# Storing the last tile but one in two transfers of 1024 columns instead of four of 512

## The chip, the cores and the metric

One core of a Trainium2 chip runs the whole program. The metric is the device time of one execution in microseconds (us); the kernel before has a median of 319.64 us over four runs (319.51 to 319.73).

## The reference

The kernel adds to x (8 batches of 512 tokens, 2048 features, float32) the output of a routed low-rank layer. Its input is a linear layer with a low-rank adapter chosen for each batch; of the 8 experts, each token takes only the one with the highest logit, times that logit. Cut to what matters:

```python
# conditioning: x is (8, 512, 2048), W is (2048, 2048)
base_out = einsum('bti,oi->bto', x, W) + b
lora_h   = einsum('bti,bir->btr', x, lora_As[mapping])
y        = base_out + 2.0 * einsum('btr,bro->bto', lora_h, lora_Bs[mapping])
# routed low-rank layer: 8 experts of rank 16, best one only
logits = einsum('bsd,ed->bse', y, route_w)
topk_v, topk_idx = top_k(logits, 1)
route_weight = one_hot(topk_idx[..., 0], 8) * topk_v
h   = einsum('bsd,erd->bser', y, A)
out = x + einsum('bser,eor->bso', route_weight[..., None] * h, Bw)
```

## The kernel before

The layers in front of the routing are folded into one small matrix first: W times the 136 columns of A and of the router (128 of the experts, 8 logits), and for each batch the adapter's part is added. After that, each token needs only a product of its 2048 features with a 2048 x 136 matrix, the choice of the expert, and a product of 128 values with the 128 x 2048 matrix `fb`.

The 4096 tokens are 32 tiles of 128 rows (`NT` = 32), loaded in pairs (`TPU` = 2) into buffers of 128 x 2 x 2048. For each tile:

- POOL and ACT shuffle the loaded rows into quarters, and VectorE (DVE) transposes 32 x 32 blocks (`shuffle`, line 249, and `turn_x`, line 234).
- TensorE multiplies the 16 transposed blocks with the folded matrix (`heads`, line 452).
- DVE picks the expert and scales its 16 values (`route`, lines 463 to 473).
- TensorE transposes that (`turn_heads`, line 520), ACT copies it to SBUF (`keep_heads`, line 525).
- TensorE multiplies it with `fb`, 512 columns to a matmul (`delta`, line 558); DVE adds the product to the tile of x in place (`add_delta`, line 571); the tile is stored from there (`store`, line 580).

The order on each engine is the order in which the program issues the work. The loop at line 606 runs over half tiles: pass n computes half of tile n // 2's heads and the `delta` of an earlier half (`piece(n)`), and adds the half before that. A `delta` of one half is 1024 columns.

For tiles 0 to 29 a half is one PSUM tile of 1024 columns, added by one instruction, and the tile is stored whole (128 rows of 8 KB) after its second half. The last two tiles are listed in `ends` (line 536). Their halves are cut into pieces, each with a PSUM bank of its own, `pe_o`, `pe_h` or `pe_s` by the pool it is from:

```python
    ends = {
        (NT - 2, 0): (("o", 512), ("o", 512)),
        (NT - 2, 1): (("h", 512), ("s", 512)),
        (NT - 1, 0): (("h", 512), ("o", 512)),
        (NT - 1, 1): (("o", 512), ("h", 256), ("s", 256)),
    }
```

Each piece is added and stored by itself, so tile 30 leaves in four stores of 512 columns and tile 31 in three of 512 and two of 256. All stores of tile 30 are issued by SP; those of tile 31 by SP and ACT in turn within a half. `add_delta` may be told to handle only the first n pieces of a half; that is done once, at line 640, where the first piece of tile 30 is added one pass before the second. `po_tiles[t, h]` keeps the pieces that are still to be added.

SP issues all loads of x and nearly all stores, in program order. By line 606's last passes all loads have been issued. A store waits on SP for the DVE add of its columns, and then goes out. No later instruction of the kernel writes the columns of tile 30 again.

Of the kernel before, what the change touches and what calls it, by code (L numbers as in the profile page):

```python
# [18 lines left out]
def kernel(  # L19
# [32 lines left out]
    nc = tc.nc  # L52
# [3 lines left out]
    B, T, D = x.shape  # L56
# [9 lines left out]
    NT = B * TPB  # L66
# [369 lines left out]
    po_tiles = {}  # L436
# [90 lines left out]
    def bank(tag, n):  # L527
# [8 lines left out]
# [6 lines that stand above are left out]
# [22 lines left out]
    def add_delta(t, h, n=None):  # L564

        u, k = divmod(t, TPU)
        pieces = po_tiles[t, h]
        po_tiles[t, h] = pieces[n:] if n else []
        for m, (cols, part) in enumerate(pieces[:n]):
            xs = x_tiles[u][:, k, cols]  # L570
            nc.vector.tensor_tensor(xs, xs, part, ALU.add)  # L571
            if (t, h) in ends:
                store(t, cols, nc.scalar if t == NT - 1 and m % 2 else nc.sync)
            elif h == 1:
                store(t, ds(0, D))

    def store(t, cols, eng=nc.sync):
        u, k = divmod(t, TPU)
        b, r = divmod(t, TPB)
        eng.dma_start(out=out[b, ts(r, P), cols], in_=x_tiles[u][:, k, cols])  # L580
# [25 lines left out]
    for n in range(2 * NT + 4):  # L606
        t, h = divmod(n, 2)
# [7 lines left out]
        if tp >= 0 and not folds(n - 1):  # L615
            add_delta(tp, hp)
# [11 lines left out]
        if folds(n):  # L628
            pass
        elif n == 2 * NT:  # L630

            delta(*piece(n), lambda: turn_heads(t - 1))
        else:
            if folds(n - 1):
                delta(*piece(n - 1))
                add_delta(*piece(n - 1))
            if piece(n)[0] >= 0:
                delta(*piece(n))
            if n == 2 * NT - 1:
                add_delta(*piece(n), 1)  # L640
# [54 lines left out]
```

## Time and profile before

| what | value |
|---|---|
| median of 4 runs | 319.64 us (319.51 to 319.73) |
| the profiled execution's own time | 319.53 us |
| its span in the profile | 317.8 us |
| TensorE (PE) busy | 311.3 us, 98% |
| DVE / ACT / POOL busy | 239.4 / 188.1 / 163.5 us |
| HBM read / written | 54.60 / 33.55 MB |
| granted TensorE clock, mean | 1.0 |

The page's list of transfers, by line, engine, count, size of one and median time from issue to landing:

```profile
x<-in_x_dram SPq DMA_DIRECT2D x32, 1024.0 KB, 8.0
out_dram<-x SPq DMA_DIRECT2D x30, 1024.0 KB, 4.7
...
out_dram<-x SPq DMA_DIRECT2D x6, 256.0 KB, 2.6
...
out_dram<-x ACTq DMA_DIRECT2D x1, 256.0 KB, 2.4
```

The 30 stores of 1024 KB are tiles 0 to 29. Six of the 256 KB stores on SP and one on ACT are the pieces of tiles 30 and 31 with 512 columns; a row of such a piece is 2 KB in each of 128 partitions. A row of a whole tile is 8 KB. The program ends when all stores have landed.

### The profile page before, as it was taken

The page shows a single profiled execution, that of the slowest core. Times are in us where ns is not written, and L with a number is a line of the kernel's source. Part 1 is how long each engine was busy: PE and PEld are TensorE (multiplying, and loading weights), DVE is VectorE, ACT ScalarE, POOL GpSimd, SP SyncE. Part 2 cuts the span into 40 slices and gives each one's busy share as a digit, 9 for nine tenths or more (in the row PEclk, how much of TensorE's full clock was granted, in tenths as well). Part 3 has the DMA queues.
Part 4 walks back from the last instruction along what each step waited for, and adds up shares of the span by engine and source line. Part 5 has one row for each costly group of instructions (what it writes and reads, how often), then busy time and mean ns, then how long its engine had stood idle before and what let it go on. Part 6 is the DMA issues. An engine that isn't in the chain of part 4 may idle for free.

```text
span 317.8 us, 5569 instructions
## 1 busy us (share of the span) xinstructions
PE 311.3 (98%) x2140; PEld 246.1 (77%) x2140; DVE 239.4 (75%) x422; ACT 188.1 (59%) x245; POOL 163.5 (51%) x167
## 2 busy tenths in 40 slices
PE   7999999999999999999999999999999999999994
PEld 7999999999776767786777767767777777677762
DVE  2221699957988798879887987888888888888864
ACT  3322366848697497659765965677587749760000
POOL 1012095999994849094819553935397276710000
PEclk9999999999999999999999999999999999999999
DMA  7999999989323494959495858767685859444337
GB/s 283 410 363 415 419 421 422 416 323 403 142 101 165 168 362 173 375 205 385 146 399 187 352 170 359 249 282 257 273 325 206 329 231 363 168 168 169 162 149 249
DMA packets 15307, 88.52 MB, mean 279 GB/s; under 512 B 1696, under 2 KB 4016, under 8 KB 4912
## 3 DMA queue, kind: packets, MB, share of 16 engines
q1 hardware_dynamic: 14112, 85.45, 68.6%
q0 software_dynamic: 320, 2.11, 1.6%
q10 hardware_dynamic: 848, 0.61, 0.6%
q8 instruction: 17, 0.28, 0.4%
q14 instruction: 10, 0.08, 0.1%
HBM read 54.60 MB, written 33.55 MB: 277 GB/s over the span
## 4 chain that ended last, share of the span: by engine, by line
PE 96%; DMA 2%; DVE 1%; DVEq 0%; issue 0%
PE ph L452 38%; PE po L558 32%; PE pc L293 19%; DMA w<-in_w_dram 2%; PE po L349 2%; PE pg L333 1%; PE pw L520 1%; PE pe_o L558 1%; PE ph L349 1%; PE pe_h L558 1%; DVE x L571 0%; PE pc L349 0%; PE pe_s L558 0%; DVE m L370 0%; DVE wv L279 0%; DVEq L691 0%
## 5 line engine op out<-in xcount | busy, mean ns | idle before, releaser
L249 POOL COPY xq<-x 32x1024 f32<-32x1024 f32 x121 | 126.4, 1044 | 77.3 <-DVE wh L473 32.4
L249 ACT COPY xq<-x 32x1024 f32<-32x1024 f32 x135 | 140.9, 1043 | 14.7 <-DMA x<-in_x_dram 12.7
L452 PEld LDWEIGHTS ph<-m,xT 128*128 128x128 f32 x1024 | 124.8, 190 | 21.1 <-issue 15.8
L452 PE MATMUL ph<-m,xT 128*128 128x136 f32 x1024 | 129.7, 280 | 0.3 <-DVE m L370 0.3
L558 PE MATMUL po<-fb,whT 128*128 128x512 f32 x240 | 111.6, 592 | 0.0
L571 DVE TENSOR_TENSOR x<-x,po 128x1024 f32<-128x1024 f32 x60 | 72.9, 1216 | 28.2 <-PE po L558 27.9
L234 DVE STREAM_TRANSPOSE xT<-xq 128x1024 f32<-128x1024 f32 x64 | 78.8, 1235 | 2.4 <-POOL xq L249 1.8
L558 PEld LDWEIGHTS po<-fb,whT 128*128 128x128 f32 x240 | 41.7, 190 | 32.0 <-issue 31.8
L293 PE MATMUL pc<-pj,wv 128*128 128x136 f32 x512 | 59.9, 279 | 0.7 <-DVE wv L279 0.7
L293 PEld LDWEIGHTS pc<-pj,wv 128*128 128x128 f32 x512 | 59.5, 190 | 0.9 <-DVE wv L279 0.9
L525 ACT COPY whT<-pw 128x128 f32<-128x128 f32 x32 | 8.5, 265 | 56.9 <-PE pw L520 56.8
L279 ACT COPY wv<-w 128x1024 f32<-128x1024 f32 (+1 forms) x17 | 16.8, 996 | 30.1 <-DMA w<-in_w_dram 28.8
L279 DVE COPY wv<-w 128x1024 f32<-128x1024 f32 (+1 forms) x17 | 13.0, 771 | 25.6 <-DMA w<-in_w_dram 20.4
L515 POOL TENSOR_TENSOR m<-m,c 128x408 f32<-128x408 f32 x14 | 14.4, 1048 | 1.6 <-ACT m L510 1.1
L221 POOL COPY ad_q<-ad_ar 32x512 f32<-32x512 f32 x12 | 8.9, 744 | 9.6 <-DMA ad_ar<-in_cond_a_dram,arow_i 9.0
L508 DVE TENSOR_TENSOR m<-c,po 128x408 f32<-128x408 f32 x14 | 7.5, 575 | 5.2 <-PE po L349 5.2
L504 ACT COPY m<-ph 128x136 f32<-128x136 f32 x14 | 3.1, 275 | 13.8 <-PE pa L349 13.8
L463 DVE TENSOR_TENSOR ph<-ph,c0b 128x136 f32<-128x136 f32 x32 | 9.0, 282 | 1.8 <-PE ph L452 1.8
L391 POOL DMA_DIRECT2D bias_o<-in_bias_dram x1 | 0.7, 735 | 18.6 <-DVE bias_o L390 18.6
L520 PEld LDWEIGHTS pw<-ident,wh 128*128 128x128 f32 x32 | 4.5, 141 | 7.4 <-issue 7.2
L473 DVE TENSOR_TENSOR wh<-ph,rw 128x128 f32<-128x128 f32 x32 | 9.3, 291 | 1.1
L471 DVE TENSOR_SCALAR rw<-ph,win,top 128x8 f32<-128x8 f32 x32 | 9.1, 284 | 1.2
(70 smaller groups left out, 146.6 us busy)
## 6 DMA issues: line engine op xcount, KB each, us to landing
x<-in_x_dram SPq DMA_DIRECT2D x32, 1024.0 KB, 8.0
out_dram<-x SPq DMA_DIRECT2D x30, 1024.0 KB, 4.7
w<-in_w_dram SPq DMA_DIRECT2D x16, 1024.0 KB, 11.9
out_dram<-x SPq DMA_DIRECT2D x6, 256.0 KB, 2.6
fb<-in_ffn_b_dram SPq DMA_DIRECT2D x1, 1024.0 KB, 12.6
pj<-in_proj_dram SPq DMA_DIRECT2D x2, 272.0 KB, 12.3
out_dram<-x ACTq DMA_DIRECT2D x1, 256.0 KB, 2.4
pj<-in_proj_dram SPq DMA_DIRECT2D x1, 204.0 KB, 9.4
```

Source lines behind the costliest of these rows:

```text
L234: nc.vector.transpose(dst[:, ts(h, HJ), :].rearrange("p j (g t) -> p g j t", t=Q), src.rearrange("p g (j a) -> p g j a", a=Q)[:, :, ts(h, ...
L249: copy(xq_tiles[u][ts(i, Q), :, g, :], x_tiles[u][ts(g, Q), :, ts(i, DQ)])
L279: copy(dst[:, ts(k, n)], wr[:, ds(h * HJ + k * n, n)])
L293: nc.tensor.matmul(pcs[z][:, n, :], wv_tiles[oc, j // HJ][:, j % HJ, :], pj[:, oc, :], start=(oc == 0 and n == 0), stop=(oc == NO - 1), sk ...
L349: nc.tensor.matmul(out, ad_q[ts(q, Q), b // 2, n, :], g4[ts(q, Q), b, :], start=start, stop=True, skip_group_check=not start, tile_positio ...
L452: nc.tensor.matmul(ph_tiles[t][:, :NP], xT_tiles[t][:, j, :], place(m, (j,))[:, 0, :], start=(j == 0), stop=(j == NJ - 1),)
L463: nc.vector.tensor_tensor(ph, ph, c0b, ALU.add)
L471: nc.vector.tensor_scalar(rw, key, win, top, ALU.is_equal, ALU.mult)
L473: nc.vector.tensor_tensor(wh.rearrange("p (e r) -> p e r", r=R), ph[:, :ER].rearrange("p (e r) -> p e r", r=R), rw.unsqueeze(2).to_broadca ...
L515: nc.gpsimd.tensor_tensor(place(m, js), place(m, js), place(cs, js), ALU.add)
L558: nc.tensor.matmul(part, whT_tiles[t], fb[:, ds(c, n)], start=True, stop=True)
L571: nc.vector.tensor_tensor(xs, xs, part, ALU.add)
```

## The change

Tile 31 is stored as before, piece by piece, on SP and ACT in turn. For tile 30 the four pieces are still computed and added one by one, but a store is issued only after the last piece of a half, and it covers the half: 1024 columns, 512 KB, rows of 4 KB, on SP. The condition asks that no piece of the half is left to be added and that this is its last one; so the piece that is added early at line 640 issues nothing. The other tiles' stores stay.

```diff
@@ -569,9 +569,11 @@
         for m, (cols, part) in enumerate(pieces[:n]):
             xs = x_tiles[u][:, k, cols]
             nc.vector.tensor_tensor(xs, xs, part, ALU.add)
-            if (t, h) in ends:
-                store(t, cols, nc.scalar if t == NT - 1 and m % 2 else nc.sync)
-            elif h == 1:
+            if t == NT - 1:
+                store(t, cols, nc.scalar if m % 2 else nc.sync)
+            elif (t, h) in ends and not po_tiles[t, h] and part is pieces[-1][1]:
+                store(t, ds(h * D // 2, D // 2))
+            elif (t, h) not in ends and h == 1:
                 store(t, ds(0, D))
```

## The prediction

> **What bounds the kernel now.** I read the page's chain first, then the end of the chain, then the last 10 us instruction by instruction, then the transfers of that stretch in quarter microseconds.
>
> The page: the profiled execution, and who stands on the chain that ends last.
>
> ```profile
> span 317.8 us, 5569 instructions
> ...
> PE 96%; DMA 2%; DVE 1%; DVEq 0%; issue 0%
> ```
>
> TensorE sets the time until its last matmul. The change touches neither a matmul nor what feeds one, so only what follows the last matmuls can move. Those last pieces of the chain are:
>
> ```profile
> 312.51 0.02 issue
> 312.54 1.02 DVE x L571 x2
> 313.56 0.33 DVEq L691
> ```
>
> The printed chain stops at 313.56 + 0.33 = 313.89 us, yet the span is 317.8. The 3.9 us after it hold no compute; what runs there is the last store. So the end is read from the stores. The adds that release the stores of the last tile but one (tile 30), and the issues of all stores of tiles 30 and 31 (start, length, engine):
>
> ```profile
> 307.96 1.27 DVE L571 TENSOR_TENSOR x<-x,pe_o 128x512 f32<-128x512 f32 x2
> 309.15 0.68 DVE L571 TENSOR_TENSOR x<-x,pe_h 128x512 f32<-128x512 f32 x1
> 309.96 0.69 DVE L571 TENSOR_TENSOR x<-x,pe_s 128x512 f32<-128x512 f32 x1
> ...
> 308.66 0.33 SPq L580 DMA_DIRECT2D out_dram<-x  x1
> 309.26 0.33 SPq L580 DMA_DIRECT2D out_dram<-x  x1
> 309.86 0.33 SPq L580 DMA_DIRECT2D out_dram<-x  x1
> 310.68 0.33 SPq L580 DMA_DIRECT2D out_dram<-x  x1
> 311.54 0.33 SPq L580 DMA_DIRECT2D out_dram<-x  x1
> 312.40 0.35 ACTq L580 DMA_DIRECT2D out_dram<-x  x1
> 313.25 0.33 SPq L580 DMA_DIRECT2D out_dram<-x  x1
> 313.59 0.35 ACTq L580 DMA_DIRECT2D out_dram<-x  x1
> 313.91 0.33 SPq L580 DMA_DIRECT2D out_dram<-x  x1
> ```
>
> The first four issues are tile 30 (I call them c0 to c3), the next five tile 31 (d0 to d4; d3 and d4 are 256 columns wide). The trace of the line gives their times from issue to landing: c0 2.4 us, c2 3.0, c3 2.7, d0 2.5, d1 2.4, d4 2.9. The last lands at 313.91 + 2.9 = 316.8, and closing the program takes the other 1.0 us to 317.8. A 256 KB store that meets nothing in its way needs 2.4 us (c0, d1); the smaller d4 needs 2.9, so at least 0.5 us of it is queueing. That is where an earlier store can reach the end. The transfers in stretches (the last two columns are the busy share of the 16 DMA engines, and GB/s; a share a little over 1 is a full engine whose packets overlap):
>
> ```profile
> 306.50:309.00 2.50, 2.50 (x8) 1.11 (x7) 2.33 (x8) 0.00 (x0) 0.00 (x0) 1.00 1.01 419
> 309.25:309.50 0.25, 0.25 (x2) 0.03 (x1) 0.25 (x1) 0.17 (x1) 0.00 (x0) 1.00 0.02 8
> 309.50:313.00 3.50, 3.50 (x11) 1.87 (x10) 2.86 (x5) 0.00 (x0) 0.00 (x0) 1.00 1.04 349
> 311.00:313.00 2.00, 2.00 (x8) 1.14 (x6) 1.66 (x3) 0.00 (x0) 0.00 (x0) 1.00 1.03 332
> 313.00:313.25 0.25, 0.25 (x2) 0.00 (x0) 0.25 (x2) 0.00 (x0) 0.00 (x0) 1.00 0.68 254
> 314.00:314.25 0.25, 0.00 (x0) 0.00 (x0) 0.00 (x0) 0.00 (x0) 0.00 (x0) 1.00 0.71 230
> ```
>
> Three things are to be seen. The DMA engines stand idle until 309.50, which is 0.84 us after the issue of c0: that is the time from an issue to its first data. From 309.50 they are full, at 349 GB/s for rows of 2 KB, where the store of tile 29 with rows of 8 KB ran at 419. And twice, at 313.0 and 314.0, they run dry for a moment: when d1 and d2 come, the queue is empty. What happens to tile 30 is therefore almost forgotten before the end, by a margin of a few tenths.
>
> **The change, part by part.** Both stores of tile 30 stay on SP, in the same places of its queue.
>
> *Removed:* two issues of 0.33 us on SP, and 256 of the 512 row packets of tile 30. SP is between waits for DVE there (it stands free from 308.66 + 0.33 = 308.99 to 309.26), so the issues are worth nothing. Without that cover, each would be worth at most its 0.33 us.
>
> *The wait that is added:* the store of the first half (call it A) now waits for the second add instead of the first. It is issued at 309.26, 0.60 us after c0. Queued behind it on SP are the second half (B) and the last tile's stores; B goes at 310.68, where c3 went, and waits for its own add anyway. No engine waits for SP: the tile's buffer isn't loaded again. The first matmul piece of tile 30, which is added early and alone, has no store of its own any more; that is the same 0.60. The adds and ACT's copies keep their times.
>
> *Transfer time.* By the full stretch, 256 KB take 262 KB / 349 GB/s = 0.75 us. No row of 4 KB stands in the trace, so the 512 KB of A is bounded from both sides: at the 2 KB rows' 349 GB/s it takes 1.50 us, at the 8 KB rows' 419 it takes 1.25. With a time per byte that is a constant and a cost per packet, 2 KB rows need 2.865 us per MB and 8 KB rows 2.387; the cost per packet at 8 KB is a third of the difference, 0.159, and at 4 KB twice that, so 2.387 + 0.159 = 2.546 us per MB and 1.33 us for 512 KB. I take 1.33.
>
> The Trainium skill speaks against any gain from longer rows: its page "DMA: Bandwidth & Descriptors", section "Where 436 GB/s comes from", says that between HBM and SBUF the HBM side binds at about 358 GB/s per core. The 419 GB/s of this trace's 8 KB rows stand above that, so the measurement decides; by the page the estimate for 512 KB would be 1.46 us and the sum below +0.47 instead of +0.26.
>
> *The queue, before:* data can start 0.84 us after each issue, and each 256 KB takes 0.75. c0 309.50 to 310.25, c1 to 311.00, c2 to 311.75, c3 to 312.50, d0 to 313.25, d1 to 314.00, d2 (can start 314.09) to 314.84. The two dips just where d1 and d2 start agree.
>
> *After:* A can start at 309.26 + 0.84 = 310.10 and ends 311.43. B can start at 311.52 and ends 312.85. d0, ready since 312.38, ends 313.60; d1 314.35; d2, ready since 314.09, ends 315.10. That is 0.26 us behind 314.84. d3 and d4 queue right behind d2 in both kernels, so the last landing and the end come 0.26 us later. The 0.60 us of the late start and 0.09 us of gap between A and B are paid back by 2 x (1.50 - 1.33) = 0.34 us of cheaper packets and by 0.09 us of slack before d2: 0.60 + 0.09 - 0.34 - 0.09 = 0.26.
>
> With 1.50 us for A: A ends 311.60, B 313.10, d2 315.35, so +0.51. With 1.25: B 312.77, d2 315.02, so +0.18. Below that the bound is about nothing: if d1 and d2 still meet an empty queue, the end is as before. A gain could come only from d2 to d4 being cheaper, and they are unchanged.
>
> The profiled execution has a span of 317.8 and took 319.53; with +0.26 it would be 319.79. The median of the four runs shown, 319.64, stands 0.11 above that execution, and the forecast is for a median: 319.64 + 0.26 = 319.90.
>
> **The rivals.** *Hidden altogether:* the queue is dry twice before the end, and if 512 KB go as fast as the best quarter microseconds of tile 29 (524 GB/s, 1.00 us), A ends 311.10, B 312.52, d2 314.86: +0.02, so 319.66. For it: the dips. Against it: 524 is a rate of quarters that others of 295 follow.
>
> *Slower:* the 4 KB rows don't go faster than the slowest full stretch shown, 332 GB/s over 311 to 313. Then A and B take 1.58 us each, B ends 313.26, d2 315.51: +0.67, so 320.31. It decides from 1.565 us per half (335 GB/s) on, where the sum reaches +0.64, which is 0.2%. For it: with a backlog nothing pays back the late start, and the two dips are means over 16 engines at 0.68 and 0.71, so some engines were busy all through them. Against it: the average row says 349, and longer rows have never been slower here.
>
> *Faster:* if all queueing of d4 vanished, its 2.9 us would become 2.4 at best, 0.5 us, so 319.14. For it: half the packets of tile 30. Against it: d2 to d4 themselves put 512 KB into the queue in 0.66 us, so they queue whatever tile 30 does. Even all of it isn't 0.2%.
>
> **How the numbers follow.** A measurement of this kernel can tell about 0.2%, 0.64 us, from no change; the bounds are 319.00 and 320.28. Forecast (+0.1 to +0.6) 0.52, hidden 0.19, slower 0.24, faster beyond 0.64 0.05. The first two lie within the bound and make 0.71. The range 319.5 to 320.45 takes in the bounds +0.18 and +0.51 and the slower rival's 320.31, with a little under the hidden case; the forecast's own range is 319.75 to 320.25.
>
> **What would show it right or wrong.** Right: A issued at about 309.26 and B at 310.68, the idle stretch of the DMA engines about 0.6 us longer, GB/s between 349 and 419 for A and B, no dips at 313.0 and 314.0 any more, d0 and d1 landing some 0.3 us later after issue than their 2.5 and 2.4, d4 about 0.3 later than its 2.9. Wrong: dips still there (hidden), or A and B at 335 GB/s or less and d4 landing 3.5 us or more after its issue (slower). If any matmul before 312 has moved, the whole reading is wrong.

## The result, and the profile after

The changed kernel takes 319.91 us (median of 40 runs, 319.70 to 320.32) against 319.61 of the kernel before on the same chips (60 runs, 319.42 to 319.89). The ratio is 1.001, 95% interval [1.0006, 1.0015]: slower by 0.30 us, between 0.2 and 0.5. So small a difference shows only over this many runs: it is half of the 0.2% that the prediction took for what can be told from no change.

The page of the changed kernel shows the same chain from the folding matmuls on, with a span 0.3 us longer, and the two stores that replace four:

```profile
span 318.1 us, 5565 instructions
...
PE 98%; DVE 1%; DVEq 0%; issue 0%
...
out_dram<-x SPq DMA_DIRECT2D x2, 512.0 KB, 2.6
out_dram<-x SPq DMA_DIRECT2D x2, 256.0 KB, 2.9
out_dram<-x ACTq DMA_DIRECT2D x1, 256.0 KB, 2.8
```

Of the stores of 256 KB that are left, d0 and d2 on SP have a median of 2.9 us to landing where c0 to d2 had 2.6, and d1 on ACT 2.8 where it had 2.4. They wait in a queue that was all but empty before. The issues of the changed kernel, in order: A, B, d0 to d4 (start, length, engine).

```profile
309.19 0.33 SPq L582 DMA_DIRECT2D out_dram<-x  x1
310.60 0.33 SPq L582 DMA_DIRECT2D out_dram<-x  x1
311.46 0.33 SPq L582 DMA_DIRECT2D out_dram<-x  x1
312.32 0.35 ACTq L582 DMA_DIRECT2D out_dram<-x  x1
313.18 0.33 SPq L582 DMA_DIRECT2D out_dram<-x  x1
313.51 0.35 ACTq L582 DMA_DIRECT2D out_dram<-x  x1
313.84 0.33 SPq L582 DMA_DIRECT2D out_dram<-x  x1
```

B and everything after it stand 0.08 us earlier than their counterparts before. That is the whole body of this execution: its first folding matmul (line 293) began at 6.32 us instead of 6.39. Over all profiles of this study it lies between 6.32 and 6.64, and the 307.5 us from there to the end of the last add are the same to some hundredths in all but two of them (0.1 and 0.2 longer). So tenths are best read from the last issue on. The transfers of the changed kernel by stretches (last two columns: busy share of the DMA engines, GB/s):

```profile
309.25:310.00 0.75, 0.75 (x3) 0.38 (x2) 0.62 (x2) 0.10 (x1) 0.00 (x0) 1.00 0.00 0
311.50:312.75 1.25, 1.25 (x6) 0.72 (x5) 0.98 (x2) 0.00 (x0) 0.00 (x0) 1.00 1.00 400
313.00:313.25 0.25, 0.25 (x2) 0.00 (x0) 0.25 (x2) 0.00 (x0) 0.00 (x0) 1.00 1.01 385
314.00:314.25 0.25, 0.00 (x0) 0.00 (x0) 0.00 (x0) 0.00 (x0) 0.00 (x0) 1.00 1.12 377
314.25:316.00 1.75, 0.00 (x0) 0.00 (x0) 0.00 (x0) 0.00 (x0) 0.00 (x0) 1.00 0.95 280
```

The engines now idle until 310.0 instead of 309.50; B's 4 KB rows go at 400 GB/s; and the two dips at 313.0 (0.68 before) and 314.0 (0.71) are gone. The backlog reaches the end.

But the end has a second part. The trace's records of landings put the last one at 316.78 before and 316.96 after. From there to the end of the span are 0.98 us before and 1.10 after. This is SP in that last stretch, from the last landing on, first before, then after:

```profile
L691 SPq EVENT_SEMAPHORE  x4: 17/22/28, 316.8 to 317.7; - x4
```

```profile
L693 SPq EVENT_SEMAPHORE  x6: 17/28/28, 317.0 to 318.0; - x6
```

Two of each belong to the final barrier. The others are waits for the completion semaphores of the stores: two follow the last landing before, four after, each about 0.06 us after the one before it (the first of them is the wait that the last landing ends). Last issue to last landing went from 2.87 to 3.12 us (+0.25), the closing from 0.98 to 1.10 (+0.12), the body from 313.91 to 313.84 (-0.08): together the +0.30 of the span, 317.76 to 318.06.

### The profile page after: what moved, and what is told of

It reads as the page before. It is cut to its first block, busy times and chain, and to the rows that moved or that the text cites. A ratio compares the mean times of both kernels' runs of the same rounds, so it can differ in the third digit from the quotient of the medians.

```text
span 318.1 us, 5565 instructions
## 1 busy us (share of the span) xinstructions
PE 312.0 (98%) x2140; PEld 246.9 (78%) x2140; DVE 239.4 (75%) x422; ACT 188.0 (59%) x245; POOL 163.4 (51%) x167
## 4 chain that ended last, share of the span: by engine, by line
PE 98%; DVE 1%; DVEq 0%; issue 0%
PE ph L452 38%; PE po L558 32%; PE pc L293 19%; PE pm L133 2%; PE po L349 2%; PE pg L333 1%; PE pw L520 1%; PE pe_o L558 1%; PE ph L349 1%; PE pe_h L558 1%; DVE x L571 0%; PE pc L349 0%; PE pe_s L558 0%; DVE m L370 0%; DVEq L693 0%; PE pb L325 0%
```

## The experiments

Two readings were to be told apart: the queue theory of the prediction (a late start, whose backlog is carried on), and a cost of merged stores by themselves. A third, on the closing, came up on the way. Each run was timed beside the kernel before on the same chip, 5 to 11 runs against 15 to 33. The intervals of the ratios are about 0.1% wide to each side, 0.3 us, so differences of a tenth or two are not settled by the times; the last stretch of each trace is what tells them apart. All together, the difference of the medians, and from the traces the time from the last issue to the last landing (transfers) and from there to the end (closing), in us:

| kernel | stores of tiles 30 and 31 | time against before, 95% of the ratio | transfers | closing |
|---|---|---|---|---|
| before | 9 | | 2.87 | 0.98 |
| changed | 7 | +0.30 [1.0006, 1.0015] | 3.12 | 1.10 |
| first half merged | 8 | +0.15 [0.9997, 1.0015] | 2.91 | 1.04 |
| second half merged | 8 | +0.23 [0.9998, 1.0016] | 3.04 | 1.04 |
| pairs issued late | 9 | +0.02 [0.9992, 1.0011] | 2.86 | 0.98 |
| tile 30 in one store | 6 | +1.59 [1.0040, 1.0067] | 4.20 | 1.17 |
| tile 30 not stored | 5 | +0.19 [0.9995, 1.0013] | 2.73 | 1.23 |
| changed, d0 not stored | 6 | -0.04 [0.9991, 1.0009] | 2.72 | 1.17 |
| last two pieces merged | 8 | -0.22 [0.9985, 1.0003] | 2.59 | 1.04 |
| changed, two more loads | 7 | +0.35 [1.0001, 1.0019] | 3.12 | 0.98 |
| before, two more loads | 9 | +0.13 [0.9994, 1.0012] | 2.76 | 1.21 |
| pairs in reverse order | 9 | +0.30 [0.9999, 1.0017] | 3.04 | 0.98 |
| last two merged, two loads | 8 | -0.42 [0.9977, 0.9995] | 2.56 | 0.92 |
| last two merged, three loads | 8 | -0.07 [0.9987, 1.0005] | 2.50 | 1.21 |

Where two kernels issue the same stores, their traces show how far one profile can be trusted: 2.87, 2.86 and 2.76 for those of before, 3.12 twice for those of the changed kernel.

**First half merged.** Only columns 0 to 1023 of tile 30 are one store.

```diff
-            if (t, h) in ends:
+            last = not po_tiles[t, h] and part is pieces[-1][1]
+            if (t, h) == (NT - 2, 0):
+                if last:
+                    store(t, ds(0, D // 2))
+            elif (t, h) in ends:
```

> Only the first half of tile 30 is one store of 1024 columns; its second half stays two stores of 512. Queue theory (a late start whose backlog is carried to the last store; 0.84 us to first data, 0.75 us for 256 KB, 1.33 us for 512 KB): A from 310.10 to 311.43, c2 to 312.18, c3 to 312.93, d0 313.68, d1 314.43, d2 315.18, against 314.84 before: +0.34 us, at least as much as both halves merged (+0.26). Rival (each merged store costs something by itself, whatever the queue does): half of what both cost, about +0.15 us.

+0.15 us, with 0.06 in the closing and 0.04 in the transfers of the trace. The time falls on the rival's number, but the trace doesn't bear it out: A is as late, and the second half's two stores queue behind it as the theory has it (the trace's packet records put the first data of d0 at 312.75, against 312.52 before). The delay of 0.27 us there, counted from the body's shift, shrank to 0.04 at the last landing. A miss for the theory's end, not for its beginning.

**Second half merged.** The same for columns 1024 to 2047 alone, with `(NT - 2, 1)` and `ds(D // 2, D // 2)` in those lines.

> Only the second half of tile 30 is one store of 1024 columns. Queue theory: c0 and c1 end at 311.00 as before, then the DMA engines wait for the merged store until 311.52; it ends 312.85, as with both halves merged, so d2 ends 315.10: +0.26 us, the whole loss, although only one half is merged. Rival (each merged store costs something by itself): half of the loss, about +0.15 us.

+0.23 us: 0.17 in the transfers, 0.06 in the closing. d0's first data came at 312.80, 0.27 late, as far as with both halves merged (0.29). One merge does nearly what two do, because B's data start about 0.83 us after its issue whatever went ahead: at 311.51 here, after the engines had run dry, and at 311.45 in the changed kernel.

**Pairs issued late.** Four stores of 512 columns, those of a half both written in the program after its second add.

```diff
+            if t == NT - 2:
+                if last:
+                    for c in range(2):
+                        store(t, ds(h * D // 2 + 512 * c, 512))
-            if (t, h) in ends:
+            elif (t, h) in ends:
```

> Tile 30 keeps four stores of 512 columns, but each waits until its half is complete: c0 and c1 go one behind the other after the second add, c2 and c3 after the fourth. Queue theory: the late start stays and the cheaper 4 KB rows are gone: from 310.10 c0 to 310.85, c1 to 311.60, c2 to 312.35, c3 to 313.10, d2 to 315.35: +0.51 us, about twice the loss of the merged stores. Rival (the loss comes from the size of the merged stores): no loss, 0.0 us.

The number is the rival's, but the run says nothing for it. This is SP in that trace:

```profile
308.74 0.33 SPq L585 DMA_DIRECT2D out_dram<-x  x1
309.33 0.33 SPq L585 DMA_DIRECT2D out_dram<-x  x1
309.93 0.33 SPq L585 DMA_DIRECT2D out_dram<-x  x1
310.75 0.33 SPq L585 DMA_DIRECT2D out_dram<-x  x1
```

These are the four issues of the kernel before, 0.07 us later with the whole body. A store waits on SP for the add of its own columns, not for its place among DVE's instructions; the edit changed nothing. It can stand as a repetition of the kernel before. What makes the merged store late is that its columns include the second piece.

**Tile 30 in one store.** The change in a larger dose: 2048 columns after the fourth add (`if last and h == 1: store(t, ds(0, D))`).

> Tile 30 is one store of 2048 columns after its fourth add. Queue theory: it can start at 311.52, needs 2.50 us at 419 GB/s and ends 314.02; d0 314.77, d1 315.52, d2 316.27: +1.43 us, since nothing after it runs the queue dry. Rival (each merged store costs something by itself, and the queue forgets tile 30 before the end): +0.15 to +0.3 us.

+1.59 us: 1.33 in the transfers, 0.19 in the closing. The backlog grows as the theory says, and a fixed cost of a merged store is out.

**Tile 30 not stored.** The stores of tile 30 are left out, so its rows of the output are not written.

> Kernel before without any store of tile 30 (its output is left out). Queue theory: d1 and d2 already met an empty queue before, so taking 1 MB out of it gains next to nothing: 0.0 to -0.15 us. Rival (the end still feels tile 30's stores in the kernel before, so there was more to win by making them cheaper): -0.3 us or more.

+0.19 us, within the noise of the times, and in any case no gain from 1 MB less of stores. In the trace the transfers gained 0.14, the end of the range that the theory gave, and the closing lost 0.25. The queue of the kernel before was indeed near empty at the end; and the closing grows when stores are taken away.

**The changed kernel without d0.** Columns 0 to 511 of tile 31 are not stored (`if (h, m) != (0, 0)` ahead of its store).

> The changed kernel without the first store of tile 31 (its columns 0 to 511 are left out), so that 0.75 us of work go out of the queue between the merged stores and the end. Queue theory: B ends 312.85, d1 starts on its own time at 313.24, d2 at 314.09 and ends 314.84 as before: the loss is gone, 0.0 us against the kernel before. Rival (the merged stores cost something by themselves, or the closing of the program does): the loss of +0.3 us stays.

-0.04 us, in spite of a closing 0.19 longer than before: the transfers took 2.72. That is what they took with no store of tile 30 at all (2.73): with 256 KB less between the merged stores and the end, nothing of the late start is left. The merged stores delay the last landing only through the queue behind them.

**Last two pieces of tile 31 merged.** Tile 30 as before; the last 512 columns go out after the last add, on SP.

```diff
-            if (t, h) in ends:
+            if (t, h) == (NT - 1, 1) and m:
+                if m == 2:
+                    store(t, ds(D - 512, 512))
+            elif (t, h) in ends:
```

> Kernel before, but the last two pieces of tile 31 (256 columns each) go out as one store of 512 columns after the last add; tile 30 is stored as before. Queue theory: d3 could start at 314.43 but waits for d2 until 314.84 anyway, and the merged store can start at 314.75; 256 KB in rows of 2 KB need 0.75 us, so data end 315.59. In the profile of before the data end about 316.0, as 1 KB rows move at 274 GB/s: -0.2 to -0.4 us. Rival (merging loses here as it does in tile 30, since its first part waits): +0.1 to +0.3 us.

-0.22 us: -0.28 in the transfers, +0.06 in the closing. The time alone doesn't settle it (the interval reaches 1.0003), but all three traces with this merge have shorter transfers, 2.50 to 2.59. The same merge that loses in tile 30 gains here. In the kernel before, the first of the two pieces stood in a queue anyway (its first data came at 314.78, 1.19 us after its issue), so its wait costs nothing, while 128 rows of 2 KB replace 256 of 1 KB.

**Two more loads.** The closings in the table so far follow the number of stores exactly: 0.98 for nine, and 0.06 more for each store fewer. To move the count without touching a store, two small loads were put on SP some passes before the end.

```diff
+        if n == 2 * NT - 8:
+            for z in range(2):
+                spare = const.tile([P, B], I32, name=f"spare_{z}")
+                nc.sync.dma_start(out=spare, in_=itok.to_broadcast([P, B]))
         if h == 0 and 1 < t < NT:
             turn_heads(t - 1)
```

In the changed kernel:

> The changed kernel with two more loads of 4 KB (the batch indices again, into spare tiles) on SP a few passes before the end. The profile of the changed kernel shows four semaphore instructions of SP after the last landing where the kernel before shows two; each takes 0.06 us. Theory of the closing (the semaphores of the transfers go round in turn, and the program ends by waiting for them in a fixed order, so fewer stores put the last one earlier in that order): with two more transfers the count is two again, the closing 0.98 us instead of 1.10, the time 0.12 us under the changed kernel, about 0.18 us over the kernel before. Rival (the closing has nothing to do with the number of transfers): no change, +0.30 us over the kernel before.

In the kernel before:

> The kernel before with the same two more loads. Theory of the closing: the last store's semaphore goes round to the front of the order, five instructions follow it instead of two: closing 0.98 + 3 x 0.06 = 1.16 us, time +0.19 us over the kernel before, with all stores of the last two tiles issued and landing as there. Rival (closing independent of the number of transfers): 0.0 us.

The closings came out as the theory has them, 0.98 and 1.21 us. The times don't settle it: the second, +0.13, is near the +0.19 forecast, but its interval takes in no change; the first came to +0.35 and not +0.18, over a wide spread (319.54 to 320.31). In its profile the transfers are 3.12 as in the changed kernel and the closing is shorter, while the body began 0.32 us later, before any of the edited work. Why its median isn't lower stays open.

**Pairs in reverse order.** What the late pairs were meant to be: `for c in (1, 0)` in that loop, so that the second piece's store is ahead in SP's queue and holds the first back.

> Tile 30 keeps four stores of 512 columns, but in each half the second is issued ahead of the first, so that the first really waits on SP behind it (in the kernel with each pair issued after the second add, the first store was not held back: it waits for its own data alone). Queue theory: c1 at 309.26, c0 right behind, c3 at 310.68, c2 behind; with 0.75 us each from 310.10 they end 313.10, d2 315.35: +0.51 us, about twice the queue's part of the merged stores, and the same closing as before. Rival (the loss comes from the size of the merged stores): 0.0 us.

SP's issues in that trace, two to a line:

```profile
309.47 0.81 SPq L585 DMA_DIRECT2D out_dram<-x  x2
310.88 0.82 SPq L585 DMA_DIRECT2D out_dram<-x  x2
```

+0.30 us, of which 0.17 show in the transfers with the closing unchanged. Neither theory has this number. The trace has a late start and longer transfers with rows and sizes as before, so it isn't the size of the stores; it is the late start. But 0.17 is a third of the 0.51 expected. The transfers of this kernel say where the rest went:

```profile
310.25:313.25 3.00, 3.00 (x10) 1.52 (x8) 2.48 (x4) 0.00 (x0) 0.00 (x0) 1.00 1.03 346
313.75:315.25 1.50, 0.00 (x0) 0.00 (x0) 0.34 (x2) 0.00 (x0) 0.00 (x0) 1.00 1.05 395
```

Tile 30 moves at 346 GB/s, as forecast, and d0's first data come at 313.28, 0.55 late after the body's shift of 0.21. Then tile 31's stores move at 395, and 0.55 becomes 0.17. So a backlog can be worked off. How far is seen in the 1.5 us from 314.00 on, by the same columns, in the changed kernel, with the first half merged, and with the second half merged:

```profile
314.00:315.50 1.50, 0.00 (x0) 0.00 (x0) 0.00 (x0) 0.00 (x0) 0.00 (x0) 1.00 1.07 328
```

```profile
314.00:315.50 1.50, 0.00 (x0) 0.00 (x0) 0.00 (x0) 0.00 (x0) 0.00 (x0) 1.00 1.04 369
```

```profile
314.00:315.50 1.50, 0.00 (x0) 0.00 (x0) 0.00 (x0) 0.00 (x0) 0.00 (x0) 1.00 1.08 329
```

The engines are full in all three. At 369 GB/s (388 with the reversed pairs) 0.23 and 0.38 us of the lateness at d0 go away, at 328 and 329 only 0.04 and 0.10.

The traces also show where the slow rate falls, though no experiment was made for it. In an unbroken run of 2 KB rows, the first 1.5 us go at 359 to 377 GB/s and the next half microsecond at 262 to 311, with the engines full. The run begins with d0 in the changed kernel (312.74) and with c2 where only the first half is merged (311.33):

```profile
312.74:314.24 1.50, 0.55 (x3) 0.14 (x1) 1.07 (x3) 0.00 (x0) 0.00 (x0) 1.00 1.04 369
314.24:314.74 0.50, 0.00 (x0) 0.00 (x0) 0.00 (x0) 0.00 (x0) 0.00 (x0) 1.00 1.12 307
```

```profile
311.33:312.83 1.50, 1.50 (x6) 0.87 (x5) 1.16 (x3) 0.00 (x0) 0.00 (x0) 1.00 1.03 369
312.83:313.33 0.50, 0.49 (x3) 0.08 (x1) 0.50 (x2) 0.00 (x0) 0.00 (x0) 1.00 1.08 307
```

By the packet records it is the 257th to 320th packet of the run, the beginning of its third store: they take 116 to 127 ns on average, where the groups of 64 ahead of them take 83 to 103. This is so in all twelve kernels whose run gets that far, and not where the engines run dry ahead of the third store (tile 30 not stored: 86 to 88). So in the changed kernel and with the second half merged, the slow stretch falls on d2, close to the end; with the first half merged and with the reversed pairs, it is over before 314.00. That is about half of the gap between 328 and 369: from 314.24 to 314.74 the changed kernel moves 307 GB/s and the one with the first half merged 381, from 314.74 to 315.50 it is 322 and 363. The second half of the gap, and why the third store is slow, stay open.

**Last two merged, with two and with three loads.** Both edits together, which by the theory leave one wait from the last landing on with two loads, and send the last store to the front of the order with three.

> The kernel before with the last two pieces of tile 31 as one store, and the two more loads. Queue theory as in the run without these loads: -0.2 us. Theory of the closing on top: one semaphore instruction after the last landing instead of three there, -0.12 us, so -0.3 us under the kernel before. Rival (closing independent): -0.2 us as without the loads.

> As the kernel before with the last two pieces of tile 31 as one store, but with three more small loads instead of two. Nothing else differs from the run with two, whose time was 0.42 us under the kernel before and whose closing took 0.92 us. Theory of the closing: the third load sends the last store's semaphore to the front of the order, so five more semaphore instructions follow the last landing, 5 x 0.06 = 0.31 us: closing about 1.2 us, time about 0.1 us under the kernel before. Rival (the gain of the run with two loads came from the loads or from the merged store alone): the same time as with two, 0.4 us under the kernel before.

-0.42 us and -0.07 us, each against the kernel before on its own chip. One more load of 4 KB, long done when the tail begins, goes with 0.35 us of the median. SP from the last landing on with two loads (one wait and the two of the barrier), and with three (six waits, the first of them the one of 2.1 us that the last landing ends, and the two of the barrier):

```profile
L698 SPq EVENT_SEMAPHORE  x3: 17/17/28, 316.8 to 317.7; - x3
```

```profile
L698 SPq EVENT_SEMAPHORE  x8: 17/28/2087, 314.6 to 317.8; - x8
```

The closings are 0.92 and 1.21 us, 0.29 apart; that is the part of the 0.35 that the traces show to come from the load. The version with two loads is the fastest of the study, 319.15 us against 319.57, ratio 0.9986 [0.9977, 0.9995].

## Why the prediction was right

It forecast 319.90 and 319.91 was measured; the direction and the place were right too. As differences it is +0.26 against +0.30: the forecast stood on a median of four runs, 319.64, and the 60 runs of the kernel before have 319.61. By its own steps:

- *The place.* Right: no matmul and no add moved but with the body, and all of the difference lies behind the last issue.
- *The late start of A, 0.60 us after c0.* Right: A took the place of c1, and its first data came at 310.01, 0.83 us after its issue (forecast 0.84).
- *512 KB in 1.33 us.* Nearly: in the packet records A has its first data at 310.01, B 311.45, d0 312.74, so B took 1.29 (with the first half merged, A too took 1.29, from 310.04 to the first 2 KB row at 311.33). The interpolation between rows of 2 and 8 KB holds for 4 KB. This is also where the slower rival fell: it needed 335 GB/s or less, and B went at 400. The page of the Trainium skill "DMA: Bandwidth & Descriptors", section "Where 436 GB/s comes from", names about 358 GB/s of the HBM side as what binds; the stores of this core exceed it with 4 KB rows as well.
- *d0 late by 0.35.* Measured 0.29 after the body's shift. The dips went, so the change was not hidden altogether.
- *One queue for all stores.* The sum lined up the stores of SP and ACT one behind the other. In the packet records they share the engines: in the changed kernel d2's data begin at 314.12, while d1's run to 314.35. What this does to the sum wasn't separated.
- *Each store of tile 31 takes 0.75 us, so that nothing but 0.09 us of slack pays back the rest.* This is the mis-sized term. The first two stores of a run of 2 KB rows go faster, about 369 GB/s, and the third begins slower, at 307. In the changed kernel this happened to cost nothing: 0.29 at d0 became 0.25 at the last landing, where 0.26 was forecast. In the experiments the same step failed: 0.27 became 0.04 with the first half merged, where +0.34 was expected, and 0.55 became 0.17 with the reversed pairs, where +0.51 was. There tile 31's stores went at 369 and 388 GB/s in the stretch from 314.00, in the changed kernel at 328. About half of this gap is the slow half microsecond of the run, which fell on d2 in the changed kernel; the rest, and why that stretch is slow, stay open.
- *Closing the program takes the other 1.0 us.* Taken as fixed, and wrong by 0.12 us. Two stores fewer put the last one two places earlier in the order in which SP waits for completion semaphores.
- *Two side sums.* By the prediction's own steps, 1.46 us for 512 KB gives d2 at 315.27, +0.43 and not +0.47, and 1.00 us gives d2 at 314.84, +0.00 and not +0.02. The forecast uses neither.

So the sum of +0.26 met a median of +0.30 with one term of 0.12 missing; the trace's own tail, 0.25 + 0.12 = 0.37, is 0.07 above the median's difference, inside its interval. The hit to a hundredth is luck: a missing term and a base 0.03 too high went against each other. So in part is the size, since with the first half merged a backlog nearly as long shrank on its way. The sign and the late start behind it are not.

## What to carry to other kernels

Near the end of a kernel, ask of each store whether the queue in front of it is empty when it could first go: if so, merging it with a later piece delays data by the wait (tile 30, +0.25 us in the transfers); if it would queue anyway, merging saves packets at no cost (the last two pieces, -0.28). A backlog made several stores before the end is not a fixed loss: of 0.27 to 0.55 us at the last tile's first store, 0.04 to 0.25 were left at the end (with tile 30 in one store, 1.33 of 1.52). And a store's place in the program isn't its time of issue: it waits for the data that it covers, or for what stands ahead of it in its queue.

## What the runs showed of the hardware

The time between the last landing and the end of the program depends on how many transfers came before. SP waits for the completion semaphores in a fixed order, and in these traces the transfers take eight of them in turn; each wait behind the one for the last landing costs 0.06 us, although long fulfilled. The closing was 0.92 us with one wait from the last landing on, 0.98 with two, 1.04, 1.10, 1.17 and 1.23 with one more each (1.21 in the two runs where the first of six had begun long before). One more load of 4 KB lengthened the closing by 0.29 us in this way; the medians, on two chips, stood 0.35 apart.

Stores in rows of 2 KB don't keep one rate: behind each other without a gap, they went at 359 to 377 GB/s for 1.5 us and at 262 to 311 for the half microsecond after it.
